# Cross-attention over 16 batches: the steps of the last batches are put in the order of all the others

## The chip, the cores and the metric

The kernel runs on one core of a Trainium2 chip, as one program with one launch. The metric is the device time of that program in microseconds (us), as the median of repeated runs. A profile of one execution stands beside it; its span is the time from the first to the last recorded instruction on the core.

## The reference

There are 16 batches. Each has 256 queries of width 256 (`x`) and 77 context rows of width 192 (`c`). There are 8 heads of width 256, all in fp32.

```
Q = x @ Wq ; K = c @ Wk ; V = c @ Wv               # split into 8 heads
score = Q K^T / sqrt(256), masked keys set to -inf
attn  = softmax(score)                             # over the 77 keys
out   = (attn V, heads side by side) @ Wo + x
result = (out - mean) * rsqrt(var + 1e-5) * gamma + beta     # per row of 256
```

## The kernel before

**Tiling.** A tile is 128 queries; a batch `b` has the two tiles `t = 2b` and `2b+1`, so there are 32 tiles, 0 to 31. The weights are folded ahead of the loop: Wq with Wk per head into `gA`, `gB`, and Wv with Wo per head into `uA`, `uB`. What is left per batch is, on TensorE (PE): `scores` (two tiles, L313), the folded values `vw` of the batch (`prepare_vw`, L241 and L252), the folded keys `a` of a later group of four batches (`prepare_a`, L199 and L213; only while such a group is left), and the weighting of the values by the softmax, which writes the output tile `po`.

**The chain of one tile.** `scores` fills two PSUM banks `ps`. `shift` adds the mask bias on VectorE (DVE), one instruction per bank (L328), and takes the maximum of each head (`top`, L335). `exponential` runs on ScalarE (ACT). `weigh` sums the exponentials (`den`, L355) and inverts the sum (`rden`, L357) on DVE, and multiplies on GpSimd (POOL, L363, two instructions) into a block `p`, of which there are two. `turn` transposes `p` on DVE into `pT` (L373). The weighting matmuls read `pT`. `add_product` adds `po` to the row of `x` on DVE (L483). `finish` takes the statistics (`bn`, L491, and `mv`, L494), `spread` takes the square root on ACT (`std`, L502), and `invert` its inverse on DVE (`rstd`, L509). `normalise` has two forms. By itself it is two DVE instructions (L531, L534). With `aside=True` it is one ACT instruction (L527), which needs a small value `less` from POOL (L513), and two POOL multiplications and additions (`gam` L528, `bet` L529).

**The loop** runs over `b` from -1 to 15. A step issues `scores` of the tiles `new` (batch b+1), the weighting of the tiles `now` (batch b), and the normalisation of the tiles `old` (batch b-1). Each engine runs its instructions in the order in which the code issues them; no scheduler moves them. `NS` is 11.

- For b below `NS` the order is: scores, shift, matmuls of `vw` and `a`; then for each new tile exponential, finish of an old tile, weigh; then the square root, the copies of `vw` and `a` out of PSUM, the weighting with seven products instead of eight (`seven`, L436), a tiny exponential named `warm` that brings ACT's table back to the exponential, invert, normalise, turn, normalise.
- From b = 11 on (batches 12 to 15 being new) the weighting is the plain one (`attend`, L385) and the order is another one. The old tiles are added, finished and square-rooted early in the step, before the new tiles are shifted (after it where b is 11). The maximum is not given to the exponential: POOL subtracts it from the whole tile (L337), and one exponential over 616 elements follows (L346) in place of eight over 77. The `vw` copies stand between the two exponentials, and both tiles are turned at the end of the step.
- After the loop come tiles 28 to 31: 28 and 31 are normalised on DVE, 29 and 30 with `aside`.

PSUM has eight banks in one rotation. From b = 11 on a step takes eight of them: four `ps`, two `pv` (the values, before the copy) and two `po`. The output DMAs are all issued by SyncE (SP), in the order of the code: one for each pair of tiles, and one each for tiles 30 and 31.

Of the kernel before, what the change touches and what calls it, by code (L numbers as in the profile page):

```python
# [10 lines left out]
AF = mybir.ActivationFunctionType  # L11
ALU = mybir.AluOpType
AX = mybir.AxisListType
PSUM = bass.MemoryType.PSUM

P = 128
H = 8
# [36 lines left out]
def kernel(  # L54
# [13 lines left out]
    nc = tc.nc  # L68
    B, S, DI = x.shape
# [5 lines left out]
    QT = S // P  # L75
# [155 lines left out]
    def prepare_vw(b):  # L231

        vw_of[b] = vwp.tile([P, 4, 2, P], F32, tag="vw", name=f"vw_{b}", bufs=3)
        parts = slice(0, 4) if b < NS else slice(1, 5)
        pv = []

        def part_A():
            for k in range(2):
                pv.append(ps_mm.tile([P, 2 * DI], F32, tag="mm", name=f"pv_{b}_{k}"))
                for i in range(NM):  # L240
                    nc.tensor.matmul(  # L241
                        pv[k][i * BK : (i + 1) * BK],
                        cA[:, b, k * BK : (k + 1) * BK],
                        uA[:, parts, :, i],
                        start=True,
                        stop=False,
                    )

        def part_B():
            for i in range(NM):  # L250
                for k in range(2):
                    nc.tensor.matmul(  # L252
                        pv[k][i * BK : (i + 1) * BK],
                        cB[half(k), b, k * BK : (k + 1) * BK],
                        uB[half(k), parts, :, i],
                        start=False,
                        stop=True,
                    )

        def copies():  # L260
            return [
                (vw_of[b][:, :, k, :], pv[k].rearrange("p (q d) -> p q d", q=4)) for k in range(2)
            ]

        return part_A, part_B, copies
# [56 lines left out]
    def shift(t):  # L322


        b, ps = t // QT, ps_of.pop(t)
        s = sp.tile([P, H, S2], F32, tag="s", name=f"s_{t}")
        for a in range(2):
            nc.vector.tensor_tensor(  # L328
                s[:, a * H // 2 : (a + 1) * H // 2],
                ps[a][:, : H // 2 * S2].rearrange("p (h k) -> p h k", k=S2),  # L330
                bias[:, b, :].unsqueeze(1).to_broadcast([P, H // 2, S2]),
                ALU.add,
            )
        top = st.tile([P, H], F32, tag="top", name=f"top_{t}")
        nc.vector.tensor_reduce(top, s, AX.X, ALU.max, negate=t // QT <= NS)  # L335
        if t // QT > NS:
            nc.gpsimd.tensor_tensor(  # L337
                s, s, top.unsqueeze(2).to_broadcast([P, H, S2]), ALU.subtract
            )
        s_of[t] = s, top  # L340

    def exponential(t):
        e = sp.tile([P, H, S2], F32, tag="e", name=f"e_{t}")
        s, top = s_of.pop(t)
        if t // QT > NS:
            nc.scalar.activation(e, s, AF.Exp)  # L346
        else:
            for h in range(H):
                nc.scalar.activation(e[:, h], s[:, h], AF.Exp, bias=top[:, h : h + 1])  # L349
        e_of[t] = e  # L350

    def weigh(t):
# [128 lines left out]
    def add_product(t):  # L481
        y = xg_of[t // GT][:, t % GT, :]
        nc.vector.tensor_tensor(y, po_of.pop(t), y, ALU.add)  # L483

    def finish(t):
        if t in po_of:
            add_product(t)
        g, j = t // GT, t % GT
        y = xg_of[g][:, j, :]
        bn = st.tile([P, 6], F32, tag="bn", name=f"bn_{t}")  # L490
        nc.vector.bn_stats(bn, y)  # L491
        if j == 0:
            mv_of[g] = st.tile([P, GT, 2], F32, tag="mv", name=f"mv_{g}", bufs=2)
        nc.vector.bn_aggr(mv_of[g][:, j, :], bn)  # L494
# [3 lines left out]
    def spread(first, last):  # L498

        g, lo, hi = first // GT, first % GT, (last - 1) % GT + 1  # L500
        std = st.tile([P, GT], F32, tag="std", name=f"std_{first}")
        nc.scalar.activation(std[:, lo:hi], mv_of[g][:, lo:hi, 1], AF.Sqrt, bias=eps)  # L502
        std_of[first, last] = std

    def invert(first, last, aside=False):

        g, lo, hi = first // GT, first % GT, (last - 1) % GT + 1
        rstd = st.tile([P, GT], F32, tag="rstd", name=f"rstd_{first}")
        nc.vector.reciprocal(rstd[:, lo:hi], std_of.pop((first, last))[:, lo:hi])  # L509
        if aside:  # L510
            less = st.tile([P, GT], F32, tag="less", name=f"less_{first}")
            for j in range(lo, hi):
                nc.gpsimd.tensor_scalar(  # L513
                    less[:, j : j + 1], mv_of[g][:, j, 0:1], rstd[:, j : j + 1], -1.0,
                    ALU.mult, ALU.mult,
                )
        for t in range(first, last):
            j = slice(t % GT, t % GT + 1)
            rstd_of[t] = rstd[:, j], less[:, j] if aside else None
# [315 lines left out]

    assert QT == 2
    last = NT - 1
    for b in range(-1, B):
        old = range(max(b - 1, 0) * QT, b * QT)
        now = range(max(b, 0) * QT, (b + 1) * QT)  # L840
        new = range((b + 1) * QT, min(b + 2, B) * QT)
        for t in new:
            scores(t)
        if old and new and b > NS:
            for t in old:
                finish(t)
            spread(old[0], old[-1] + 1)
        for t in new:
            shift(t)
        if b == NS:  # L850
            for t in old:
                finish(t)
            spread(old[0], old[-1] + 1)
        for n in range(0, 2) if b < 0 else range(b + 2, min(b + 3, B // 2)):
            turn_last(n)
        if b >= NS and new:
            invert(old[0], old[-1] + 1, aside=True)
        g, n = (b + 1) // GB + 1, (b + 1) % GB
        work = []
        if b + 1 < B:  # L860
            work.append(prepare_vw(b + 1))
        if g < NG:
            work.append(prepare_a(g, (n,)))
            if n == 0:
                load_xT(g)
                load_x(g)
        for part_A, _, _ in work:
            part_A()
        for _, part_B, _ in work:
            part_B()  # L870
        copies = [copy for _, _, of_part in work for copy in of_part()]
        if b < NS:
            for i, t in enumerate(new):
                exponential(t)
                if old:
                    finish(old[i])
                weigh(t)
            if old:
                spread(old[0], old[-1] + 1)
            for dst, src in copies:  # L880
                nc.scalar.copy(dst, src)
            if b + 1 < NS:
                differences(b + 1)
            if now:
                seven(b)
            nc.scalar.activation(warm, eps, AF.Exp)
            if old:
                invert(old[0], old[-1] + 1)
                normalise(old[0])
            for t in new:  # L890
                turn(t)
            if n >= NF - 2:
                for j in range((n - NF + 2) * GT // 2, (n - NF + 3) * GT // 2, 2):
                    transpose_x(g, j)
            if old:
                normalise(old[1])
            if now:
                add_seven(b)
            if b + 1 < NS:
                sums(b + 1)  # L900
            continue
        for i, t in enumerate(new):
            exponential(t)
            for dst, src in copies[i : i + 1]:
                nc.scalar.copy(dst, src)
        for dst, src in copies[len(new) :]:
            nc.scalar.copy(dst, src)
        for i, t in enumerate(new):
            weigh(t)
            if old and b < B - 2 and i:  # L910
                normalise(old[i])
        for t in now:
            attend(t)
        for t in new:
            turn(t)
        if b < B - 2:
            normalise(old[0], aside=True)
        if b == B - 2:
            for i in range(QT):
                normalise(old[i], aside=True)  # L920
                finish(now[i])
            spread(now[0], now[-1] + 1)

    finish(last - 1)
    spread(last - 1, last)
    invert(last - 3, last - 1, aside=True)
    normalise(last - 3)
    invert(last - 1, last, aside=True)
    for t in range(last - 2, last):
        normalise(t, aside=True)  # L930
    finish(last)
    spread(last, NT)
    invert(last, NT)
# [32 lines left out]
```

## Time and profile before

| what | value |
|---|---|
| median of 3 runs | 284.35 us (283.92 to 285.65) |
| the profiled execution's own time | 285.26 us |
| its span | 283.5 us |
| PE busy | 271.2 us, 96% of the span |
| DVE busy | 207.5 us, 73% |
| POOL busy | 179.6 us, 63% |
| ACT busy | 156.8 us, 55% |

The page lists busy times, the span in 40 slices, the chain of work that ended last, and the costliest groups of instructions by line. A group row gives the count, the total, the mean of one in ns, and the idle time of its engine just before it with what ended it. A timeline row gives the start and length of an instruction, or of several merged ones, in us from the span's start. A merged or pipelined length can overlap the next start a little.

### The profile page before, as it was taken

Reading aid. Unit: us, or ns where it says so; the run is one execution under the profiler, and the core shown is the slowest. Engines: PE = TensorE matmul, PEld = TensorE weight load, DVE = VectorE, ACT = ScalarE, POOL = GpSimd, SP = SyncE. Lnnn points to the kernel's source line nnn. Section 1 sums busy time; section 2 is a strip of 40 time slices with the busy share of each in tenths; the row PEclk is TensorE's granted clock in tenths of the full one; section 3 lists DMA queues with packets and bytes.
Section 4 is the critical chain, followed back from the end, with each engine's and each line's share of the span. In section 5 each row is a group of like instructions: output and inputs, shape, how many; then the busy total and the mean of one; then the engine's idle time right before and its main releaser. Section 6 shows DMA issues by size and latency. Waiting matters only on the chain.

```text
span 283.5 us, 13229 instructions
## 1 busy us (share of the span) xinstructions
PE 271.2 (96%) x5925; PEld 196.8 (69%) x5925; DVE 207.5 (73%) x421; ACT 156.8 (55%) x390; POOL 179.6 (63%) x240
## 2 busy tenths in 40 slices
PE   7899999999999999999999999999999999999970
PEld 7756589985585859586858595959595957568440
DVE  0245762678738888878788888787888868898882
ACT  3212142147547676767676767676768834725641
POOL 1000049955677777787877777878777556748574
PEclk9999999999999999999999999999999999999996
DMA  5997899940000000940100009401010101010112
GB/s 186 239 225 170 258 291 232 169 133 3 2 6 2 25 19 27 201 152 3 42 2 28 16 17 214 152 5 41 4 39 4 39 5 39 3 39 5 39 38 74
DMA packets 35640, 22.60 MB, mean 80 GB/s; under 512 B 17712, under 2 KB 34048, under 8 KB 35584
## 3 DMA queue, kind: packets, MB, share of 16 engines
q1 hardware_dynamic: 35584, 21.77, 30.1%
q8 instruction: 46, 0.75, 1.1%
q14 instruction: 10, 0.08, 0.1%
HBM read 17.57 MB, written 4.19 MB: 77 GB/s over the span
## 4 chain that ended last, share of the span: by engine, by line
PE 77%; DVE 11%; POOL 4%; DMA 2%; ACT 2%; issue 2%; POOLq 0%; SPq 0%
PE ps L313 19%; PE pa L199 12%; PE po L436 9%; PE pv L241 7%; PE pm L436 7%; PE pa L213 6%; PE pv L252 4%; PE pu L683 3%; PE pr L274 2%; DMA wq_nat<-in_L_xattn_Wq_dram 2%; DVE top L335 2%; DVE s L328 2%; DVE bn L491 2%; DVE pT L373 2%; POOL p L363 1%
## 5 line engine op out<-in xcount | busy, mean ns | idle before, releaser
L349 ACT ACTIVATE e<-s,top 128x77 f32<-128x77 f32 x192 | 50.3, 346 | 42.9 <-DVE top L335 40.7
L313 PE MATMUL ps<-a,xT 128*32 128x154 f32 x2048 | 70.1, 294 | 0.0
L313 PEld LDWEIGHTS ps<-a,xT 128*32 128x32 f32 x2048 | 66.3, 110 | 1.6 <-issue 0.7
L363 POOL TENSOR_TENSOR p<-e,rden 128x512 f32<-128x512 f32 x64 | 46.7, 752 | 27.3 <-DVE rden L357 24.2
L328 DVE TENSOR_TENSOR s<-ps,bias 128x308 f32<-128x308 f32 x64 | 29.7, 473 | 14.8 <-PE ps L313 13.1
L199 PE MATMUL pa<-cA,gA 128*32 128x308 f32 x512 | 35.9, 423 | 0.4 <-ACT cA L151 0.4
L469 POOL TENSOR_TENSOR xg<-xg,m 128x256 f32<-128x256 f32 x33 | 24.2, 733 | 13.8 <-DVE xg L483 12.1
L199 PEld LDWEIGHTS pa<-cA,gA 128*32 128x32 f32 x512 | 17.0, 110 | 20.5 <-issue 7.0
L241 PE MATMUL pv<-uA,cA 128*32 128x512 f32 x256 | 30.6, 592 | 0.0
L355 DVE TENSOR_REDUCE den<-e 128x8 f32<-128x616 f32 x32 | 24.8, 776 | 7.2 <-ACT e L346 4.8
L373 DVE STREAM_TRANSPOSE pT<-p 128x640 f32<-128x640 f32 x32 | 25.5, 825 | 2.8 <-POOL p L363 2.8
L335 DVE TENSOR_REDUCE top<-s 128x8 f32<-128x616 f32 x32 | 25.4, 795 | 1.1
L671 POOL COPY cB<-cB 64x224 f32<-64x224 f32 (+1 forms) x6 | 1.9, 358 | 37.3 <-DVE cB L153 37.3
L399 POOL TENSOR_TENSOR ts<-vw 128x768 f32<-128x768 f32 x11 | 22.0, 2001 | 0.0
L385 PE MATMUL po<-vw,pT 128*32 128x256 f32 x320 | 19.2, 380 | 0.5 <-DVE pT L373 0.5
L213 PE MATMUL pa<-cB,gB 64*32 64x308 f32 x512 | 19.5, 420 | 0.0
L502 ACT ACT_TABLE_LOAD x15 | 19.2, 1283 | 0.3
L213 PEld LDWEIGHTS pa<-cB,gB 64*32 64x32 f32 x512 | 9.7, 107 | 11.3 <-issue 7.6
L337 POOL TENSOR_TENSOR s<-s,top 128x616 f32<-128x616 f32 x8 | 9.7, 1217 | 12.2 <-DVE top L335 11.0
L252 PE MATMUL pv<-uB,cB 64*32 64x512 f32 x256 | 17.4, 601 | 0.0
L385 PEld LDWEIGHTS po<-vw,pT 128*32 128x32 f32 x320 | 10.3, 110 | 10.0 <-DVE s L328 2.5
L531 DVE SCALAR_TENSOR_TENSOR xg<-xg,mv,gam 128x256 f32<-128x256 f32 x25 | 16.8, 671 | 0.0
(116 smaller groups left out, 474.7 us busy)
## 6 DMA issues: line engine op xcount, KB each, us to landing
xT<-in_x_dram SPq DMA_DIRECT2D x16, 256.0 KB, 5.7
xg<-in_x_dram SPq DMA_DIRECT2D x4, 1024.0 KB, 7.4
out_dram<-xg SPq DMA_DIRECT2D x15, 256.0 KB, 2.4
wo<-in_L_xattn_Wo_dram SPq DMA_DIRECT2D x4, 512.0 KB, 5.4
wvT<-in_L_xattn_Wv_dram SPq DMA_DIRECT2D x16, 96.0 KB, 4.0
wq_nat<-in_L_xattn_Wq_dram SPq DMA_DIRECT2D x2, 512.0 KB, 6.8
wq_blk<-in_L_xattn_Wq_dram SPq DMA_DIRECT2D x8, 128.0 KB, 4.3
wk_blk<-in_L_xattn_Wk_dram SPq DMA_DIRECT2D x8, 96.0 KB, 6.2
```

The costliest lines, as they stand in the source:

```text
L199: nc.tensor.matmul(flat(o[i * BK : (i + 1) * BK]), gA[:, h, cols(dc, i)], flat(cA[:, batches, :]), start=not B_first, stop=B_first,)
L213: nc.tensor.matmul(flat(banks[j + k][i * BK : (i + 1) * BK]), gB[half(k), h % NF, cols(dc, i)], flat(cB[half(k), batches, :]), start=B_fir ...
L241: nc.tensor.matmul(pv[k][i * BK : (i + 1) * BK], cA[:, b, k * BK : (k + 1) * BK], uA[:, parts, :, i], start=True, stop=False,)
L252: nc.tensor.matmul(pv[k][i * BK : (i + 1) * BK], cB[half(k), b, k * BK : (k + 1) * BK], uB[half(k), parts, :, i], start=False, stop=True,)
L313: nc.tensor.matmul(ps[m // 2][i * BK : (i + 1) * BK, m % 2 * 2 * S2 : (m % 2 + 1) * 2 * S2], xT_of[g][:, j * NM + m, dc], flat(a_of[g][:, ...
L328: nc.vector.tensor_tensor(s[:, a * H // 2 : (a + 1) * H // 2], ps[a][:, : H // 2 * S2].rearrange("p (h k) -> p h k", k=S2), bias[:, b, :]. ...
L335: nc.vector.tensor_reduce(top, s, AX.X, ALU.max, negate=t // QT <= NS)
L349: nc.scalar.activation(e[:, h], s[:, h], AF.Exp, bias=top[:, h : h + 1])
L363: nc.gpsimd.tensor_tensor(part, e_mh[:, :, :, keys], rden_mh.unsqueeze(3).to_broadcast(list(part.shape)), ALU.mult,)
L373: nc.vector.transpose(pT_of[t].rearrange("p n m q -> p m n q"), p.rearrange("p m (n k) -> p m n k", k=BK),)
L385: nc.tensor.matmul(po[i * BK : (i + 1) * BK], pT[:, n, i], vw_of[b][:, 2 - n // 2 * 2 : 4 - n // 2 * 2, n % 2, :] if n < NF else vr[:, b, ...
L436: nc.tensor.matmul(out[i * BK : (i + 1) * BK], weight[:, i], moving, start=(n == 0), stop=(n == len(terms) - 1),)
```

## The change

The steps with b from 11 to 14 take the order of the steps below 11, with `attend` in the place of `seven`. In them the negated maximum goes into the exponential as its bias, eight instructions per tile, and the subtraction on POOL is gone. Of the two old tiles one is normalised with `aside` and the other on DVE, as before; which of them comes first is exchanged with the order. `invert` makes `less` only for tiles normalised aside. A `warm` exponential follows in steps 11 to 13. `add_product` of the two current tiles moves to the end of the step, and their statistics to the next one. Step 14 keeps both old tiles aside and finishes the current ones. Step 15 becomes code after the loop: `attend` of tiles 30 and 31, and the end for tiles 28 to 31, of which again 28 and 31 go to DVE and 29 and 30 aside, but tile 29 is started before tile 30 is finished.

```diff
@@ shift, exponential
-        nc.vector.tensor_reduce(top, s, AX.X, ALU.max, negate=t // QT <= NS)
-        if t // QT > NS:
-            nc.gpsimd.tensor_tensor(
-                s, s, top.unsqueeze(2).to_broadcast([P, H, S2]), ALU.subtract
-            )
+        nc.vector.tensor_reduce(top, s, AX.X, ALU.max, negate=True)
...
-        if t // QT > NS:
-            nc.scalar.activation(e, s, AF.Exp)
-        else:
-            for h in range(H):
-                nc.scalar.activation(e[:, h], s[:, h], AF.Exp, bias=top[:, h : h + 1])
+        for h in range(H):
+            nc.scalar.activation(e[:, h], s[:, h], AF.Exp, bias=top[:, h : h + 1])
@@ the loop
-        if old and new and b > NS:
-            for t in old:
-                finish(t)
-            spread(old[0], old[-1] + 1)
...
-        if b == NS:
-            for t in old:
-                finish(t)
-            spread(old[0], old[-1] + 1)
...
-        if b >= NS and new:
-            invert(old[0], old[-1] + 1, aside=True)
...
+        for i, t in enumerate(new):
+            exponential(t)
+            if old:
+                finish(old[i])
+            weigh(t)
+        if old:
+            spread(old[0], old[-1] + 1)
+        for _, _, copies in work:
+            for dst, src in copies():
+                nc.scalar.copy(dst, src)
...
-        for i, t in enumerate(new):
-            exponential(t)
-            for dst, src in copies[i : i + 1]:
-                nc.scalar.copy(dst, src)
-        for dst, src in copies[len(new) :]:
-            nc.scalar.copy(dst, src)
-        for i, t in enumerate(new):
-            weigh(t)
-            if old and b < B - 2 and i:
-                normalise(old[i])
         for t in now:
             attend(t)
-        for t in new:
-            turn(t)
         if b < B - 2:
+            invert(old[0], old[-1] + 1, aside=old[:1])
             normalise(old[0], aside=True)
-        if b == B - 2:
-            for i in range(QT):
-                normalise(old[i], aside=True)
-                finish(now[i])
+            nc.scalar.activation(warm, eps, AF.Exp)
+            turn(new[0])
+            normalise(old[1])
+            turn(new[1])
+            for t in now:
+                add_product(t)
+        else:
+            turn(new[0])
+            invert(old[0], old[-1] + 1, aside=old)
+            for t in old:
+                normalise(t, aside=True)
+            turn(new[1])
+            for t in now:
+                finish(t)
             spread(now[0], now[-1] + 1)
@@ after the loop
+    for t in new:
+        attend(t)
+    invert(last - 3, last - 1, aside=(last - 2,))
+    normalise(last - 2, aside=True)
     finish(last - 1)
     spread(last - 1, last)
-    invert(last - 3, last - 1, aside=True)
     normalise(last - 3)
-    invert(last - 1, last, aside=True)
-    for t in range(last - 2, last):
-        normalise(t, aside=True)
+    invert(last - 1, last, aside=(last - 1,))
+    normalise(last - 1, aside=True)
     finish(last)
     spread(last, NT)
     invert(last, NT)
```

More of the change, by code (lines that the diff above doesn't have):

```diff
@@ L503, in spread, with invert @@
         std_of[first, last] = std
-    def invert(first, last, aside=False):
+    def invert(first, last, aside=()):
         g, lo, hi = first // GT, first % GT, (last - 1) % GT + 1
@@ L511, in invert @@
             less = st.tile([P, GT], F32, tag="less", name=f"less_{first}")
-            for j in range(lo, hi):
+            for j in (t % GT for t in aside):
                 nc.gpsimd.tensor_scalar(
@@ L837 @@
     last = NT - 1
-    for b in range(-1, B):
+    for b in range(-1, B - 1):
         old = range(max(b - 1, 0) * QT, b * QT)
         now = range(max(b, 0) * QT, (b + 1) * QT)
-        new = range((b + 1) * QT, min(b + 2, B) * QT)
+        new = range((b + 1) * QT, (b + 2) * QT)
         for t in new:
             scores(t)
-        if old and new and b > NS:
-            for t in old:
-                finish(t)
-            spread(old[0], old[-1] + 1)
         for t in new:
             shift(t)
-        if b == NS:
-            for t in old:
-                finish(t)
-            spread(old[0], old[-1] + 1)
         for n in range(0, 2) if b < 0 else range(b + 2, min(b + 3, B // 2)):
             turn_last(n)
-        if b >= NS and new:
-            invert(old[0], old[-1] + 1, aside=True)
         g, n = (b + 1) // GB + 1, (b + 1) % GB
-        work = []
-        if b + 1 < B:
-            work.append(prepare_vw(b + 1))
+        work = [prepare_vw(b + 1)]
         if g < NG:
@@ L870 @@
             part_B()
-        copies = [copy for _, _, of_part in work for copy in of_part()]
-        if b < NS:
-            for i, t in enumerate(new):
-                exponential(t)
-                if old:
-                    finish(old[i])
-                weigh(t)
-            if old:
-                spread(old[0], old[-1] + 1)
-            for dst, src in copies:
-                nc.scalar.copy(dst, src)
-            if b + 1 < NS:
-                differences(b + 1)
+        for i, t in enumerate(new):
[8 more added lines that the diff above has]
+                nc.scalar.copy(dst, src)
+        if b + 1 < NS:
+            differences(b + 1)
+        if b < NS:
             if now:
@@ L901 @@
             continue
-        for i, t in enumerate(new):
-            exponential(t)
-            for dst, src in copies[i : i + 1]:
-                nc.scalar.copy(dst, src)
-        for dst, src in copies[len(new) :]:
-            nc.scalar.copy(dst, src)
-        for i, t in enumerate(new):
-            weigh(t)
-            if old and b < B - 2 and i:
-                normalise(old[i])
         for t in now:
             attend(t)
-        for t in new:
-            turn(t)
         if b < B - 2:
+            invert(old[0], old[-1] + 1, aside=old[:1])
             normalise(old[0], aside=True)
-        if b == B - 2:
-            for i in range(QT):
-                normalise(old[i], aside=True)
-                finish(now[i])
+            nc.scalar.activation(warm, eps, AF.Exp)
[12 more added lines that the diff above has]
+                finish(t)
             spread(now[0], now[-1] + 1)
+    for t in new:
+        attend(t)
+    invert(last - 3, last - 1, aside=(last - 2,))
+    normalise(last - 2, aside=True)
     finish(last - 1)
     spread(last - 1, last)
-    invert(last - 3, last - 1, aside=True)
     normalise(last - 3)
-    invert(last - 1, last, aside=True)
-    for t in range(last - 2, last):
-        normalise(t, aside=True)
+    invert(last - 1, last, aside=(last - 1,))
+    normalise(last - 1, aside=True)
     finish(last)
```

## The prediction

> **What bounds the kernel now.** I read the busy times by stage first, because the change leaves everything before 224 us alone. The stages are the four steps with b = 11 to 14, cut where PE starts the scores of a new batch, and the end. The columns are the stretch, its length, then busy time and count of PE, PE's weight loads, DVE, ACT and POOL, the granted clock, the DMA share and GB/s.
>
> ```profile
> 224.30:235.70 11.40, 11.40 (x252) 7.40 (x246) 7.88 (x20) 6.01 (x11) 6.15 (x9) 1.00 0.08 26
> 235.70:247.05 11.35, 11.35 (x245) 7.36 (x241) 9.55 (x22) 5.80 (x9) 7.74 (x12) 1.00 0.08 26
> 247.05:258.43 11.38, 11.38 (x246) 7.36 (x241) 10.10 (x22) 5.84 (x9) 7.38 (x11) 1.00 0.08 26
> 258.43:269.81 11.38, 11.38 (x244) 7.22 (x236) 10.05 (x22) 5.85 (x9) 7.39 (x11) 1.00 0.08 27
> 269.81:283.50 13.69, 4.70 (x84) 3.02 (x80) 7.46 (x21) 3.23 (x7) 8.51 (x13) 0.84 0.16 57
> ```
>
> PE has no gap in the four steps: 11.37 us each, and no order on the other engines can make them shorter. What can change is whether PE is kept waiting, and the last 13.7 us. The next view is the timeline of PE and DVE where PE first waits.
>
> ```profile
> 269.37 0.61 PE L385 MATMUL po<-vr,pT 128*32 128x256 f32 x8
> 270.52 1.93 PE L385 MATMUL po<-vw,pT 128*32 128x256 f32 x32 [0.54 <-DVE pT L373]
> ...
> 269.53 0.84 DVE L373 STREAM_TRANSPOSE pT<-p 128x640 f32<-128x640 f32 x1
> 271.05 0.84 DVE L373 STREAM_TRANSPOSE pT<-p 128x640 f32<-128x640 f32 x1 [0.67 <-POOL p L363]
> ```
>
> The weighting of tile 30 starts 0.54 us late, as its transpose ends at 270.37. DVE is late because its own round is full: its first L328 of a step starts at 240.55 and 251.84, that is 4.9 and 4.8 us after PE began those scores at 235.67 and 247.04, though the first bank can be read after about 1.3. So in the before, DVE trails PE by about 3.5 us in the last steps. The third view is the end, on POOL and SP.
>
> ```profile
> 275.00 1.24 POOL L513 TENSOR_SCALAR less<-mv,rstd 128x1 f32<-128x1 f32 x3 [0.98 <-DVE rstd L509]
> 276.65 0.72 POOL L528 TENSOR_TENSOR xg<-xg,gam 128x256 f32<-128x256 f32 x1 [0.41 <-ACT xg L527]
> 277.45 0.95 POOL L529 TENSOR_TENSOR xg<-xg,bet 128x256 f32<-128x256 f32 x1
> 278.37 0.90 POOL L528 TENSOR_TENSOR xg<-xg,gam 128x256 f32<-128x256 f32 x1
> 279.35 0.72 POOL L529 TENSOR_TENSOR xg<-xg,bet 128x256 f32<-128x256 f32 x1
> ...
> 280.09 0.83 SPq L536 DMA_DIRECT2D out_dram<-xg  x2
> ```
>
> POOL stood idle 0.98 us for DVE's `rstd` of tiles 28 and 29 and then did tiles 29 and 30 in a row to 280.07. The two last DMA issues end at 280.92, and the span ends 2.58 us later. DVE was done with tile 31 at 278.69, so POOL's row of two tiles sets the end.
>
> The last view gives the order that the change brings in, as it already runs at b = 10 (PE began those scores at 210.19):
>
> ```profile
> 213.96 4.20 ACT L349 ACTIVATE e<-s,top 128x77 f32<-128x77 f32 x16 [3.52 <-DVE top L335]
> 218.18 1.28 ACT L502 ACT_TABLE_LOAD   x1
> 219.47 0.30 ACT L502 ACTIVATE std<-mv,eps 128x2 f32<-128x2 f32 x1
> ...
> 219.37 1.56 POOL L363 TENSOR_TENSOR p<-e,rden 128x512 f32<-128x512 f32 x2 [0.44 <-DVE rden L357]
> ...
> 219.80 0.17 DVE L509 RECIPROCAL rstd<-std 128x2 f32<-128x2 f32 x1 [0.58 <-ACT std L502]
> 219.89 0.82 DVE L531 SCALAR_TENSOR_TENSOR xg<-xg,mv,gam 128x256 f32<-128x256 f32 x1
> ```
>
> Counted from the start of the scores: exponentials from 3.77 to 7.97, `rden` of the second tile done at 9.03, `rstd` at 9.6, second `p` done at 10.74.
>
> **What the Trainium skill says.** "ScalarE: Activation LUTs", section "What ACT_TABLE_LOAD costs", gives 1283 ns for a load and 1380 ns of drain after it, and for an activation with a pointer bias 280 ns plus 0.833 ns per element, with back-to-back ones overlapping by 93 ns. For 77 elements that is 344 ns, or 251 ns apart. The trace has loads of 1283 ns, exponentials of 346 ns, and 16 of them in 4.20 us, 262 ns apart. A drain isn't seen: at 231.46 a load of 1.28 us is followed by the exponential at 232.75. The section "Table sets: the hidden batching unit" says that exp and sqrt lie in different sets and that cheap functions lie in every set. That agrees: no load stands ahead of a copy (L905) or the L527 identity. "SBUF — State Buffer", section "Who interferes with whom", says that a DVE instruction with two SBUF inputs contends with a GpSimd instruction that reads SBUF. The trace has this for L534: 0.49 us alone (236.05), 1.16 us beside `p` on POOL (247.31). PSUM inputs as in L483 and L328 aren't touched by it.
>
> **Part by part.** Per step b = 11 to 14:
>
> *Removed on POOL:* two subtractions of 1.22 us (L337) and one or two `less` of about 0.25. They stood on DVE's way to the exponential: top done, 1.23 on POOL, then the exponential.
>
> *Added on ACT:* 16 exponentials in 4.20 us for two of 0.72, so 2.8 us more. The table loads stay two per step (one in b = 14), moved. ACT's sum is 4.2 + 1.28 + 0.3 + two copies 1.05 + 0.6 + 1.28 + 0.2 = 8.9 us, below PE's 11.37. The `warm` load ends at about 11.0 (`less`) + 0.6 + 1.5 = 13.1, and the next exponential is due at 11.37 + 3.77 = 15.1, so it is hidden by 2 us; without that cover it would cost at most 1.5 per step.
>
> *Moved on DVE:* the instructions stay the same in kind and number. After `rstd` at 9.6 come turn 0.8 (10.5), L531 0.82 beside `p` (11.2), L534 0.48 (11.7; POOL has only `less` left until ACT has done L527), turn 0.8 (12.5), two additions 0.75 (13.3). So DVE is free for the next scores 1.9 us after PE starts them. The second bank comes at 2.34 (226.63 in the row of b = 11), and the first addition takes 0.38. It fits with nothing to spare: I take a lag of 0 per step, with bounds -0.1 and +0.7 (L534 at 1.16 instead of 0.48), over three steps at most 2.0.
>
> *Copies of `vw` later on ACT:* behind `std`, done at about 10.6 instead of 10.1. Their banks are needed by the next `pv` at 11.37 + 4.2 = 15.6, so nothing.
>
> *Output DMAs:* the same count and order on SP. Where a pair waits for POOL, nothing but later output stands behind it.
>
> *Step 14 and the end,* from scores at 258.42. Exponentials end at 266.39, turn of tile 30 at 268.2, `p` of 31 at 269.16, turn of 31 at 270.05. PE then starts tile 30 at 269.98 without the 0.54 us wait, and `po` of 31 is done about 0.5 earlier, at 274.5. POOL after 269.16: `less` of 26 and 27 0.5 (269.66), L527 0.6 (270.3), four L528/L529 at before's 3.05 for the four (273.35), `less` of 29 0.4 (273.75), L527 0.6 (274.4), two operations 1.75 (276.2), `less` of 30 0.3 (276.5), L527 0.6 (277.1), two operations 1.7 (278.9). Before, this was 280.07: 1.2 us earlier. DVE's tile 31 has `std` queued on ACT behind L527 of tile 30, which waits for that late `less`: 277.0 + 0.3, `rstd` 0.2, L531 0.47, L534 0.83 beside POOL, 278.8. So both ends meet at 278.9, two issues 0.83, then 2.58: the span is 282.3 instead of 283.5.
>
> The sum is -1.2 us on the profiled execution: 285.26 to 284.06. That execution lies 0.9 above the median, so I put the same difference on the median: 284.35 - 1.2 = 283.1.
>
> **Rivals.**
>
> *Given back (about 284.5).* The saved time is lost to the shared reads of DVE and POOL: L534 at 1.16 in each step gives a lag up to 2.0 by the end, 283.1 + 2.0 = 285.1 at worst, some 284.5 in the middle. For it: the before shows 1.16 in two steps out of three. Against: in the new order L534 starts after `p` is done.
>
> *Slower (about 287.5).* The new order has run only at 14.1 us per step, where PE also does `a`; the round shift, exponentials, `den`, `p`, turn, additions, next shift may need more than 11.37. Its place is DVE's first L328 in steps 12 to 14; each us of excess costs three us at the end, since POOL's last row hangs on `p` of tile 31. An excess of 1.5 gives 4.5 - 1.2 = +3.3. It decides from an excess of 0.4 (no gain left), and by 1% from 1.35. Against it: the sum above ends at 13.3, while that would need 14.7; what it would take is both L531 and L534 held for a whole `p`, besides a late `std`.
>
> *Clearly faster (about 281.2).* If POOL kept up, DVE's tile 31 alone would end it: `po` at 274.5, addition, statistics, `std`, `rstd`, two L531/L534, together 2.6, 277.1; 0.83 and 2.58 make 280.5, a gain of 3.0. Against it: after 269.66 POOL still has eight `gam`/`bet` operations of 0.73 or more, 5.8 us without a single wait, and the waits for L527 and `less` between them.
>
> *That the change doesn't do what it says* I exclude: the instruction order of the changed kernel shows the 16 exponentials, no subtraction, and the turns split around L531.
>
> **Chances.** Forecast 0.60; given back 0.20; slower 0.12; clearly faster 0.08. About 1% is what a measurement of this kernel can tell from no change, 2.8 us. The forecast and the rival given back lie within it: 0.80 same, 0.08 faster, 0.12 slower. The forecast's own bounds are 281.9 (POOL's last six operations uncontended at 0.73, and short `less`) to 283.5; with half of the faster case left out, and the given-back case taken in, the range is 281.7 to 285.2.
>
> **What would show it.** Right: PE busy without a gap to the end of the weighting of tile 31; DVE's first L328 about 1.9 to 2.3 us after each scores start from b = 12 on; 16 exponentials in 4.2 us; POOL busy from 269 on with the last `bet` at about 278.9, and std of tile 31 behind L527 of tile 30. Wrong: the first L328 drifting from step to step, PE waiting for `pT`, or POOL idle in the last 8 us while DVE or ACT is late.

## The result, and the profile after

The changed kernel takes 282.59 us (282.41 to 282.80, 5 runs) where the kernel before takes 284.49 us (283.92 to 285.65, 5 runs). The ratio is 0.9931, with a 95% interval of 0.9908 to 0.9954. It is faster by 1.9 us, or 0.7%, which lies inside the 1% called no change in the prediction; the interval of the ratio does not contain 1. The forecast was 283.1, a gain of 1.2 us.

The profiled execution has a span of 280.8 us, 2.7 less than before. Not all of that is the change: PE began the scores of batch 12 at 223.55 here and at 224.29 before, and up to there the two kernels run the same instructions. Counted from that point, before takes 283.5 - 224.29 = 59.21 us and after 280.8 - 223.55 = 57.25 us, so the changed part gained 1.96 us (the spans are given to 0.1 us), close to the 1.9 us of the medians. To compare with a time of before on one clock, 0.74 is added to a time of after.

The timeline of PE after, at the place where it waited for the transpose of tile 30 before:

```profile
268.62 0.61 PE L378 MATMUL po<-vr,pT 128*32 128x256 f32 x8
269.06 1.91 PE L378 MATMUL po<-vw,pT 128*32 128x256 f32 x32
```

There is no wait any more. 269.06 is 269.80 on the clock of before, where the same matmuls started at 270.52. The reason is on VectorE (L328 keeps its line, L373 has become L366, and L531 and L534 have become L524 and L527):

```profile
233.24 0.82 DVE L366 STREAM_TRANSPOSE pT<-p 128x640 f32<-128x640 f32 x1
233.99 0.45 DVE L524 SCALAR_TENSOR_TENSOR xg<-xg,mv,gam 128x256 f32<-128x256 f32 x1
234.47 0.48 DVE L527 SCALAR_TENSOR_TENSOR xg<-xg,rstd,bet 128x256 f32<-128x256 f32 x1
...
236.27 0.46 DVE L328 TENSOR_TENSOR s<-ps,bias 128x308 f32<-128x308 f32 x1
237.27 0.48 DVE L328 TENSOR_TENSOR s<-ps,bias 128x308 f32<-128x308 f32 x1 [0.54 <-PE ps L313]
...
259.01 0.46 DVE L328 TENSOR_TENSOR s<-ps,bias 128x308 f32<-128x308 f32 x1
260.02 0.48 DVE L328 TENSOR_TENSOR s<-ps,bias 128x308 f32<-128x308 f32 x1 [0.55 <-PE ps L313]
```

The first L328 comes 1.34 us after PE began those scores (234.93), and 1.33 us in the step of batch 15 (257.68). VectorE now waits for PE, by half a microsecond in each step. The same instructions before:

```profile
225.59 0.48 DVE L328 TENSOR_TENSOR s<-ps,bias 128x308 f32<-128x308 f32 x1
...
240.55 0.83 DVE L328 TENSOR_TENSOR s<-ps,bias 128x308 f32<-128x308 f32 x2
...
247.31 1.16 DVE L534 SCALAR_TENSOR_TENSOR xg<-xg,rstd,bet 128x256 f32<-128x256 f32 x1
...
263.12 0.83 DVE L328 TENSOR_TENSOR s<-ps,bias 128x308 f32<-128x308 f32 x2
```

Before, the first L328 came 1.30 us after the scores of batch 12 (224.29), 4.88 after those of batch 13 (235.67), 4.79 after those of batch 14 (247.04) and 4.70 after those of batch 15 (258.42). So the lag came in between two batches and was then held: VectorE's round of 11.29 us was a little shorter than PE's 11.37, but not short enough to win the lag back. What L534 was before is L527 now: 1.16 us in two of three steps before, 0.48 in every step after, because `p` is finished when it starts.

The timelines of GpSimd, ScalarE and SyncE at the end (L528 and L529 have become L521 and L522, L513 has become L506, L502 has become L495):

```profile
266.84 1.38 POOL L356 TENSOR_TENSOR p<-e,rden 128x512 f32<-128x512 f32 x2 [0.42 <-DVE rden L350]
...
272.20 0.27 POOL L506 TENSOR_SCALAR less<-mv,rstd 128x1 f32<-128x1 f32 x1
273.19 0.89 POOL L521 TENSOR_TENSOR xg<-xg,gam 128x256 f32<-128x256 f32 x1 [0.72 <-ACT xg L520]
274.15 0.72 POOL L522 TENSOR_TENSOR xg<-xg,bet 128x256 f32<-128x256 f32 x1
274.85 0.26 POOL L506 TENSOR_SCALAR less<-mv,rstd 128x1 f32<-128x1 f32 x1
275.83 0.72 POOL L521 TENSOR_TENSOR xg<-xg,gam 128x256 f32<-128x256 f32 x1 [0.72 <-ACT xg L520]
276.63 0.78 POOL L522 TENSOR_TENSOR xg<-xg,bet 128x256 f32<-128x256 f32 x1
...
275.15 0.60 ACT L520 ACTIVATE xg<-xg,less,rstd 128x256 f32<-128x256 f32 x1 [1.86 <-POOL less L506]
275.66 0.28 ACT L495 ACTIVATE std<-mv,eps 128x1 f32<-128x1 f32 x1
...
277.44 0.83 SPq L529 DMA_DIRECT2D out_dram<-xg  x2
```

The row no longer stands idle for `rstd` of tiles 28 and 29. It now waits twice for 0.72 us, each time for the round `less`, L520, `gam`. It ends at 277.41, on the clock of before at 278.15 against 280.07, and the two DMA issues follow at once.

The row as a whole did not become shorter; it starts sooner. Before, the last `p` on GpSimd is the end of this row:

```profile
268.11 2.90 POOL L363 TENSOR_TENSOR p<-e,rden 128x512 f32<-128x512 f32 x4
```

Counted from the scores of batch 15, `p` of tile 31 was done at 12.59 us before (271.01 - 258.42) and is done at 10.54 after (268.22 - 257.68), 2.05 sooner. From there to the last `bet` it took 9.06 us before and takes 9.19 after. Of the 3.37 us by which the first L328 of batch 15 comes sooner, 2.05 reach `p`; the way from L328 to `p` is 9.21 us instead of 7.89, and 0.95 of it are VectorE's two waits for PE's banks (0.55 and 0.40).

### The profile page after: what moved, and what is told of

Same layout as the page of the kernel before. It is cut to its first block, busy times and chain, and to the rows that moved or that the text cites. A ratio compares the mean times of both kernels' runs of the same rounds, so it can differ in the third digit from the quotient of the medians.

```text
span 280.8 us, 13274 instructions
## 1 busy us (share of the span) xinstructions
PE 270.8 (96%) x5925; PEld 195.6 (70%) x5925; DVE 206.1 (73%) x421; ACT 166.5 (59%) x447; POOL 168.2 (60%) x228
## 4 chain that ended last, share of the span: by engine, by line
PE 89%; POOL 2%; ACT 2%; DMA 2%; DVE 2%; issue 0%; SPq 0%; ACTq 0%; POOLq 0%
PE ps L313 23%; PE pa L199 12%; PE pv L241 9%; PE po L429 9%; PE pm L429 7%; PE pa L213 6%; PE pv L252 5%; PE po L378 5%; PE pu L676 3%; PE pr L274 2%; DMA wq_nat<-in_L_xattn_Wq_dram 2%; ACT e L342 1%; PE pg L719 1%; PE pgb L676 1%; PE pw L690 1%; PE pr L284 1%
## 5 line engine op out<-in xcount | busy, mean ns | idle before, releaser
L342 ACT ACTIVATE e<-s,top 128x77 f32<-128x77 f32 x256 | 67.1, 346 | 52.1 <-DVE top L335 49.9
L356 POOL TENSOR_TENSOR p<-e,rden 128x512 f32<-128x512 f32 x64 | 45.8, 738 | 46.6 <-DVE rden L350 46.4
L328 DVE TENSOR_TENSOR s<-ps,bias 128x308 f32<-128x308 f32 x64 | 30.3, 475 | 17.6 <-PE ps L313 15.9
L199 PEld LDWEIGHTS pa<-cA,gA 128*32 128x32 f32 x512 | 16.4, 110 | 21.1 <-issue 7.6
L366 DVE STREAM_TRANSPOSE pT<-p 128x640 f32<-128x640 f32 x32 | 25.6, 824 | 2.4 <-POOL p L356 2.4
L861 ACT COPY vw<-pv 128x512 f32<-128x512 f32 x32 | 16.9, 578 | 2.5 <-PE pv L252 2.5
L495 ACT ACT_TABLE_LOAD x14 | 18.0, 1283 | 0.3
L524 DVE SCALAR_TENSOR_TENSOR xg<-xg,mv,gam 128x256 f32<-128x256 f32 x25 | 17.1, 682 | 0.0
L861 ACT COPY a<-pa 128x308 f32<-128x308 f32 x48 | 16.6, 446 | 0.0
```

Of the source, the lines that this page charges most:

```text
L199: nc.tensor.matmul(flat(o[i * BK : (i + 1) * BK]), gA[:, h, cols(dc, i)], flat(cA[:, batches, :]), start=not B_first, stop=B_first,)
L328: nc.vector.tensor_tensor(s[:, a * H // 2 : (a + 1) * H // 2], ps[a][:, : H // 2 * S2].rearrange("p (h k) -> p h k", k=S2), bias[:, b, :]. ...
L356: nc.gpsimd.tensor_tensor(part, e_mh[:, :, :, keys], rden_mh.unsqueeze(3).to_broadcast(list(part.shape)), ALU.mult,)
L366: nc.vector.transpose(pT_of[t].rearrange("p n m q -> p m n q"), p.rearrange("p m (n k) -> p m n k", k=BK),)
```

## The experiments

The theory: the new order of the steps ends VectorE's lag behind PE, so the row of work on GpSimd begins sooner; the form of the exponential and the order of the last four tiles matter little. The rivals: the order of the last tiles gained it; the subtraction taken off GpSimd gained it; the gain is given back by contention. In the table, "end" is the span less the time at which PE began the scores of batch 15, in the profiled execution of each kernel, so that the part ahead of the change does not enter. "`p` of 31" is the time at which GpSimd has done `p` of tile 31, counted from the same scores.

| kernel | median us | ratio to before (95% interval) | `p` of 31, us | end us |
|---|---|---|---|---|
| before | 284.49 | 1 | 12.59 | 25.08 |
| the change | 282.59 | 0.9931 (0.9908 to 0.9954) | 10.54 | 23.12 |
| x1, last tiles alone | 284.09 | 0.9986 (0.9972 to 0.9999) | 12.60 | 24.73 |
| x2, steps alone | 282.63 | 0.9925 (0.9906 to 0.9944) | 10.54 | 23.33 |
| x3, subtraction in the new order | 282.56 | 0.9919 (0.9900 to 0.9938) | 10.38 | 23.09 |
| x4, bias in the old order | 294.88 | 1.0358 (1.0335 to 1.0381) | see there | see there |
| x5, square root of 31 first | 282.62 | 0.9944 (0.9925 to 0.9962) | 10.54 | 23.28 |
| x6, `less` of 30 early | 281.58 | 0.9908 (0.9892 to 0.9924) | 10.54 | 22.34 |
| x7, as x6, tile 27 on VectorE | 281.96 | 0.9917 (0.9904 to 0.9930) | 10.72 | 22.69 |
| x8, contended L524 | 282.44 | 0.9932 (0.9919 to 0.9946) | 10.53 | 23.07 |
| x9, no `warm` | 284.64 | 1.0013 (1.0003 to 1.0023) | 12.78 | 25.35 |

The end follows `p` of tile 31: less that time it is 12.49 us before, 12.58 after and 12.57 in x9. Only x6 and x7, which change the row behind `p`, are clearly below it, and x1, which does so too, a little (12.13).

**x1 and x2: the halves of the change.** x1 is the kernel before with the new code after the loop (`invert` takes the tiles for `less` as a list):

```diff
...
+    invert(last - 3, last - 1, aside=(last - 2,))
+    normalise(last - 2, aside=True)
     finish(last - 1)
     spread(last - 1, last)
-    invert(last - 3, last - 1, aside=True)
     normalise(last - 3)
-    invert(last - 1, last, aside=True)
-    for t in range(last - 2, last):
-        normalise(t, aside=True)
+    invert(last - 1, last, aside=(last - 1,))
+    normalise(last - 1, aside=True)
     finish(last)
```

> The kernel before, with only the code after the loop taken from the change (tile 29 started before tile 30 is finished, its less made apart). Theory (the new steps end VectorE's lag, and the end is worth little by itself): PE still waits 0.54 us for the transpose of tile 30, the first L328 of a step still trails by 4.8 us; GpSimd's last row starts about 1.2 us sooner but then waits for the less of tile 30, and VectorE's tile 31 waits behind tile 30 on ScalarE: about -0.5 us against before (ratio 0.998). Rival (the end is what gained): about -1.5 us or more (0.995 or less).

x2 is the changed kernel with this diff taken back.

> The changed kernel, with the code after the loop as in the kernel before. Theory: no PE wait, first L328 of each step 1.3 us after its scores, and about -1.9 us against before (0.9933), within 0.3 us of the changed kernel. Rival (the end is what gained): at most -0.7 us (0.9975).

x1 gained 0.14%, about 0.4 us, x2 0.75%. PE in x1:

```profile
269.27 1.93 PE L385 MATMUL po<-vw,pT 128*32 128x256 f32 x32 [0.54 <-DVE pT L373]
```

The 0.54 us wait is there as before, `p` of tile 31 is as late as before, and x1 ends with tile 31 on VectorE. In x2 `p` is as early as in the change. So the steps carry the gain, and the order of the last tiles adds nothing that can be measured to them. In x2 GpSimd waits 0.49 us, makes three `less` in a row (1.24 us), waits 0.41 and then runs four operations without a wait to 277.51; in the change it has two waits of 0.72. Counted from the scores of batch 15 the rows end at 19.94 and 19.73.

Which of the moves within a step ends the lag was not tried one by one. The traces let one see a part of it: before, VectorE adds and takes the statistics of two tiles between the last transposition and L328 (238.58 to 240.63, 2.05 us), after, only two additions stand there (235.63 to 236.34, 0.71 us).

**x3 and x4: the form of the exponential.** x3 is the changed kernel with the old form from batch 12 on:

```diff
-        nc.vector.tensor_reduce(top, s, AX.X, ALU.max, negate=True)
+        nc.vector.tensor_reduce(top, s, AX.X, ALU.max, negate=t // QT <= NS)
+        if t // QT > NS:
+            nc.gpsimd.tensor_tensor(
+                s, s, top.unsqueeze(2).to_broadcast([P, H, S2]), ALU.subtract
+            )
...
+        if t // QT > NS:
+            nc.scalar.activation(e, s, AF.Exp)
+        else:
+            for h in range(H):
...
```

> The changed kernel, but from batch 12 on with the maximum subtracted on GpSimd and one exponential of 616 elements per tile, as before. Theory (it is the order, not the form of the exponential): subtraction 1.22 and exponential 0.72 take as long as eight exponentials of 2.1 us, so within 0.4 us of the changed kernel, -1.5 to -2.2 us against before (0.992 to 0.995). Rival (the gain is the subtraction taken off GpSimd and off VectorE's shared reads): most of it goes, -0.7 us or less (0.9975 or more).

It is as fast as the change, 0.9919 against 0.9931. In the new order the subtraction on GpSimd costs nothing that can be measured.

x4 takes this diff the other way, in the kernel before.

> The kernel before, but with the maximum as bias and eight exponentials per tile in batches 12 to 15; the order of the steps is unchanged. Theory: the second tile's exponentials end about 1 us later than before in each step, VectorE's round of 11.3 us, which has no slack in this order, grows by up to 1 us, and the lag is carried on over three steps: +1 to +3 us (1.004 to 1.011). Rival (the subtraction was the cost): -1 us or better (0.9965 or less).

The sign was right and the size was not: +10.4 us, more than three times the upper end of what was expected. The table load before, on ScalarE:

```profile
240.98 1.28 ACT L346 ACT_TABLE_LOAD   x1
243.54 0.72 ACT L346 ACTIVATE e<-s 128x616 f32<-128x616 f32 x1 [1.27 <-POOL s L337]
```

ScalarE, VectorE and PE in x4:

```profile
242.63 0.30 ACT L495 ACTIVATE std<-mv,eps 128x2 f32<-128x2 f32 x1 [3.82 <-DVE mv L487]
244.27 1.28 ACT L342 ACT_TABLE_LOAD   x1 [1.35 <-DVE top L335]
245.56 2.11 ACT L342 ACTIVATE e<-s,top 128x77 f32<-128x77 f32 x8
247.58 0.57 ACT L898 COPY vw<-pv 128x512 f32<-128x512 f32 x1
248.04 2.11 ACT L342 ACTIVATE e<-s,top 128x77 f32<-128x77 f32 x8
...
242.51 0.83 DVE L328 TENSOR_TENSOR s<-ps,bias 128x308 f32<-128x308 f32 x2
...
279.30 3.64 PE L378 MATMUL po<-vw,pT 128*32 128x256 f32 x32 [6.56 <-DVE pT L366]
```

Two things add up in a step. The exponentials and the copy between them run from 245.56 to 250.15, 4.59 us after the load, where before the way from the end of the first `top` (242.20) through the subtractions to the end of the second exponential (245.86) was 3.66. That is the microsecond I had counted. And the table load now stands in the way: before, it ran right behind `std`, at 240.98, while the exponential waited for GpSimd. In the timeline of x4 the load itself carries the wait for `top`, so it starts when `top` is done, and its 1.28 us come on top. The loads start at 244.27 and, one step on, at 257.89, so a round takes 13.62 us where it took 11.29 before (L328 at 240.55 and 251.84). 2.33 us of excess in each step are carried on, and PE waits 6.56 us for the transpose of tile 30, besides 1.26 and 1.85 in the steps before. My 1 us in that expectation missed the load. It also missed the step of batch 12, where the load stands ahead of the exponential in both kernels: there the two exponentials and the copy between them take 4.58 us in x4 (231.95 to 236.53) and 1.81 before (232.75 to 234.56), and the first L328 of batch 13 is 2.77 us later than before. 2.77 and three times 2.33 are 9.8 of the 10.4 us. The times of x4 from the scores of batch 15 (`p` of 31 at 21.03, the end at 34.46) can't be compared with the others, as these scores themselves start late; from the scores of batch 12 it takes 69.92 us and before 59.21.

**x9: the load in the new order.** The change keeps the load away by `warm`. x9 takes it out:

```diff
-            nc.scalar.activation(warm, eps, AF.Exp)
             turn(new[0])
```

> The changed kernel without the tiny exponential (warm) at the end of steps 11 to 13. Theory: the table load for the exponential then waits together with the first exponential for the maximum, as in the run with the bias in the old order, and costs 1.35 us in steps 12, 13 and 14. VectorE has 0.6 us to spare per step: the second bank's addition is late by 0.75 in step 13 and 1.5 in step 14, p of tile 31 by 2.8, and the kernel takes about +2.8 us against the changed one (about 1.003 against before). Rival (PE sets the pace, ScalarE has room): within 0.5 us of the changed kernel (0.993 to 0.995).

Against the change it costs 1.0013/0.9931, 0.8% or 2.3 us by the ratios, and 25.35 - 23.12 = 2.2 us by the profiles: more than the whole gain, and less than the 2.8 us expected.

```profile
238.23 1.28 ACT L342 ACT_TABLE_LOAD   x1 [3.46 <-DVE top L335]
239.52 4.11 ACT L342 ACTIVATE e<-s,top 128x77 f32<-128x77 f32 x16
...
250.14 1.28 ACT L342 ACT_TABLE_LOAD   x1 [2.83 <-DVE top L335]
...
248.38 0.85 DVE L328 TENSOR_TENSOR s<-ps,bias 128x308 f32<-128x308 f32 x2
...
260.30 0.85 DVE L328 TENSOR_TENSOR s<-ps,bias 128x308 f32<-128x308 f32 x2
```

ScalarE is idle 3.46 us and then loads; the load could have run in that time. VectorE's round becomes 11.92 us (248.38 to 260.30), 0.55 more than PE's 11.37, and the lag adds up over the steps. The addition for the second bank is late by 0.55 us in step 13 and 1.09 in step 14, where 0.75 and 1.5 were expected, and `p` of tile 31 by 2.24, which is what the end loses. This is the rival called slower in the prediction: once the round is longer than PE's, the excess of each step is carried to the end, past a slack of about 0.6 us.

**x8: contention put in.** The changed kernel with VectorE's normalising ahead of both transposes:

```diff
-            turn(new[0])
             normalise(old[1])
+            turn(new[0])
             turn(new[1])
```

> The changed kernel, with VectorE's two normalising instructions ahead of both transposes in steps 11 to 13, so that L524 runs beside p on GpSimd. L524 goes from 0.45 to 0.8 us. Theory: VectorE has about 0.6 us to spare per step before it is late for the second bank, so the time stays within 0.2 us of the changed kernel, with the first L328 at 1.7 instead of 1.3 us after its scores. Rival (the gain is given back by contention): 0.4 us late per step, carried on over three steps, +1.0 us or more.

L524 went to 0.82 us in all three steps, and the time stayed: 0.9932, end 23.07.

```profile
233.48 0.82 DVE L524 SCALAR_TENSOR_TENSOR xg<-xg,mv,gam 128x256 f32<-128x256 f32 x1
...
236.87 0.46 DVE L328 TENSOR_TENSOR s<-ps,bias 128x308 f32<-128x308 f32 x1
237.52 0.48 DVE L328 TENSOR_TENSOR s<-ps,bias 128x308 f32<-128x308 f32 x1 [0.19 <-PE ps L313]
```

VectorE still waits 0.19 us for the second bank, where it waited 0.54. The slack takes in the 0.37 us that L524 became longer.

**x5, x6 and x7: what sets the end.** In x5 ScalarE takes the square root of tile 31 ahead of tile 30's L520:

```diff
-    normalise(last - 1, aside=True)
     finish(last)
     spread(last, NT)
+    normalise(last - 1, aside=True)
     invert(last, NT)
```

> The changed kernel, with the square root of tile 31 put ahead of tile 30's L520 on ScalarE. If that queueing sets the end, VectorE's rstd of tile 31 comes at 275.1 instead of 276.0 on the changed kernel's clock and the kernel gains up to 0.9 us. If GpSimd's row sets it (bet of tile 30 at 277.41, and the two last DMA issues behind it on SyncE), VectorE ends a us earlier and the time stays within 0.3 us of the changed kernel (ratio to before 0.992 to 0.995).

```profile
275.67 0.96 POOL L521 TENSOR_TENSOR xg<-xg,gam 128x256 f32<-128x256 f32 x1 [0.72 <-ACT xg L520]
...
275.57 0.48 DVE L527 SCALAR_TENSOR_TENSOR xg<-xg,rstd,bet 128x256 f32<-128x256 f32 x1
...
276.71 0.72 POOL L522 TENSOR_TENSOR xg<-xg,bet 128x256 f32<-128x256 f32 x1
...
277.46 0.83 SPq L529 DMA_DIRECT2D out_dram<-xg  x2
```

Counted from the scores of batch 15, VectorE is done at 18.53 instead of 20.02 us, and nothing is gained: the DMAs stand behind GpSimd's last `bet`, at 19.91 instead of 19.73, since `gam` of tile 30 now runs beside VectorE and takes 0.96 instead of 0.72. The chain of waits of the changed kernel ends on VectorE; that engine was last by 0.3 us and was not what held the end: the issue for tile 31 stands behind that for tile 30 on SyncE and starts at 277.89, after VectorE's 277.70.

x6 makes `less` of tile 30 between `gam` and `bet` of tile 29:

```diff
             nc.gpsimd.tensor_tensor(y, y, gam, ALU.mult)
+            if between:
+                between()
             nc.gpsimd.tensor_tensor(y, y, bet, ALU.add)
...
-    normalise(last - 2, aside=True)
-    finish(last - 1)
-    spread(last - 1, last)
-    normalise(last - 3)
-    invert(last - 1, last, aside=(last - 1,))
+
+    def while_29():
+        finish(last - 1)
+        spread(last - 1, last)
+        normalise(last - 3)
+        invert(last - 1, last, aside=(last - 1,))
+
+    normalise(last - 2, aside=True, between=while_29)
```

> The changed kernel, with less of tile 30 made between gam and bet of tile 29, so that ScalarE's L520 of tile 30 runs beside bet of tile 29. Theory (GpSimd's row of gam, bet, less sets the end): the row loses 0.7 us of waiting and the end comes 0.7 to 1.0 us sooner (about 0.990 against before). Rival (VectorE's tile 31 or the DMA issues set it): within 0.3 us of the changed kernel.

```profile
273.73 0.26 POOL L506 TENSOR_SCALAR less<-mv,rstd 128x1 f32<-128x1 f32 x1
273.95 0.72 POOL L524 TENSOR_TENSOR xg<-xg,bet 128x256 f32<-128x256 f32 x1
274.70 0.72 POOL L521 TENSOR_TENSOR xg<-xg,gam 128x256 f32<-128x256 f32 x1
275.50 0.78 POOL L524 TENSOR_TENSOR xg<-xg,bet 128x256 f32<-128x256 f32 x1
```

The second wait of 0.72 us is gone, since L520 of tile 30 runs beside `bet` of tile 29. The end comes 0.78 us sooner than in the change, and with 281.58 us (0.9908) it is the fastest kernel here. The intervals of x6 and the change overlap a little; the trace shows where the time went.

x7 adds to x6 that tile 27 is normalised on VectorE in step 14.

```diff
             turn(new[0])
-            invert(old[0], old[-1] + 1, aside=old)
-            for t in old:
-                normalise(t, aside=True)
+            invert(old[0], old[-1] + 1, aside=old[:1])
+            normalise(old[0], aside=True)
+            normalise(old[1])
             turn(new[1])
```

> As the run before (less of tile 30 between gam and bet of tile 29), and tile 27 normalised on VectorE in the idle 0.8 us ahead of the transpose of tile 31, two operations less in GpSimd's row. Theory: tile 29's gam then starts when rstd of tile 28 allows, 0.6 us sooner than 273.19, and the end comes 1.0 to 1.5 us before that of the changed kernel (about 0.988 to 0.990). Rival (the row is not what ends last): no better than the run before it, or worse by the 0.1 to 0.5 us that the transpose of tile 31 is late.

This expectation failed, and its rival came true: 0.9917, end 22.69, 0.35 later than x6. The intervals of x6 and x7 overlap, so what follows is read from the traces alone. GpSimd has two operations less and is then idle until VectorE delivers `rstd` of tiles 28 and 29:

```profile
271.79 0.26 POOL L506 TENSOR_SCALAR less<-mv,rstd 128x1 f32<-128x1 f32 x1 [0.96 <-DVE rstd L502]
272.77 0.87 POOL L521 TENSOR_TENSOR xg<-xg,gam 128x256 f32<-128x256 f32 x1 [0.72 <-ACT xg L520]
274.09 0.27 POOL L506 TENSOR_SCALAR less<-mv,rstd 128x1 f32<-128x1 f32 x1 [0.45 <-DVE rstd L502]
...
273.09 0.83 DVE L529 SCALAR_TENSOR_TENSOR xg<-xg,rstd,bet 128x256 f32<-128x256 f32 x1
```

VectorE's own work is late, as tile 27 now stands ahead of the transposition of tile 31: the first L526 of tile 28 starts 15.19 us after the scores of batch 15 (272.60 - 257.41) and in x6 at 14.83 (272.19 - 257.36). `gam` of tile 29 then meets tile 28 on VectorE (L529 0.83 instead of 0.48 in x6), so `rstd` of tile 30 is late and GpSimd waits 0.45 for it. With the row this short, VectorE holds it.

## Why the prediction was right, and where its size was off

- **PE keeps its 11.37 us per step; the gain is in VectorE's lag and in the end.** Shown. The end is the only stretch that became shorter, and it became so because `p` of tile 31 is done 2.05 us sooner.
- **VectorE late before "because its own round is full".** Only in part. A round of 11.29 us against PE's 11.37 could not win the lag back, but it did not make it either: the lag fell from 4.88 to 4.70 us. The old order had put it there once, between batches 12 and 13.
- **The 0.54 us wait goes.** Shown in the profile after, and it stays in x1.
- **VectorE free 1.9 us after the scores begin, with nothing to spare.** Too late by 0.56: it was 1.34. I had charged L531 at 0.82 us beside `p`. The first transpose stands between in the new order, and `p` took 1.38 instead of 1.56, so L524 began as `p` ended and took 0.45: 0.37 of the 0.56; the rest is in rounded lengths. The slack is about 0.6 us, not zero: the second bank comes at 2.34, two additions in a row start 0.39 apart (248.38 and 248.77 in x9), and 2.34 - 0.39 - 1.34 = 0.61. x8 shows that even 0.82 would have fitted.
- **`warm` hidden by 2 us, at most 1.5 per step without it.** Its end was put at 13.1 after the scores and the next exponential at 15.1; measured are 236.71 - 223.55 = 13.16 and 238.67 - 223.55 = 15.12. Without it, x9 lost 2.2 us in all three steps, less than the bound.
- **The end at 278.9 on the clock of before.** It was 278.15, and this 0.75 is why 1.2 became 1.9. The step of the sum that was mis-sized is GpSimd's row. Counted from the scores of batch 15: second `p` done at 10.54 (I had 10.74), first `gam` at 11.50 (11.88), fourth operation done at 14.54 (14.93), `gam` of 29 at 15.51 (15.98), its `bet` done at 17.19 (17.78), `bet` of 30 done at 19.73 (20.48). I had taken the contended rows of before for `p` (1.56) and for each last pair (1.75 and 1.7, measured 1.68 and 1.58), and a first hop from `less` to `gam` of 1.14 us that takes 0.96, as L520 starts when the first of two `less` is done. The sum also has a slip of 0.1 in it (277.1 and 1.7 are 278.8).
- **Both ends meet.** VectorE ended at 277.70 and GpSimd at 277.41. x5 shows that GpSimd's held the end.
- **The rivals.** Given back by contention: it did not happen, as L527 took 0.48 us in every step; x8 shows that 0.37 us more per step costs nothing. The 0.68 of the prediction was not tried; against the slack of 0.6 it leaves under 0.1 per step, an estimate. Slower: it did not happen, but x9 shows the mechanism, and that it was one small instruction away. Clearly faster: GpSimd's row kept it out; x6 gains 0.78 us by shortening the row, and x7 nothing more, as VectorE then holds it.
- **Readings that were off without harm.** L534 at 236.05 was not alone: the second `p` began at 236.21 beside it, and it was `p` that became longer, 1.24 us instead of 1.05. The `vw` copies are not later: the second ended 10.74 us after the scores before (235.03 - 224.29), 10.1 being its start, and ends at 10.53 after. The exponentials of a tile start 0.25 us apart; 262 ns was 4.20 us divided by 16, with the length of the last one and the step between the tiles in it.
- **What the hit is worth.** The range of 281.7 to 285.2 us contains the time of the kernel before as well: a change without any gain would have fallen into it too. What speaks for the forecast is the lag that went, the wait that went, and the two halves x1 and x2.

## What to carry to other kernels

Where PE has no gap and the other engines run their own round beside it, look at two things. One is the length of that round. If it is longer than PE's, each step's excess is carried on to the end (2.33 us in x4, 0.55 us in x9); if it is shorter, a delay that fits into the slack costs nothing (0.37 us in x8). The other is the lag. A round that is no longer than PE's can still trail far behind, as in the kernel before (11.29 against 11.37 us, and 4.7 to 4.9 us behind the scores). In the steps of that kernel it cost nothing; it was paid once, at the end, where the last row of work hung on it.

In x4 and x9 the table load cost time because it waited together with the activation that needs it; a tiny activation of the same kind ahead of the wait put the load into idle time. At the end of a kernel look for hops between engines in the row that ends last, and put the small operation that starts the hop ahead of a large one, as in x6.

## What was not expected of the hardware

The table load is not always early. In the kernel before it ran at 240.98, 2.6 us ahead of its exponential at 243.54; in x4 and x9 it started only when `top` was done and stood 1.28 us in the way. In the kernel before the exponential waited for GpSimd, in x4 and x9 for VectorE; no run here shows what decides whether the load waits too. The Trainium skill's "ScalarE: Activation LUTs", section "What ACT_TABLE_LOAD costs", has the 1283 ns, which every load here took. The 1380 ns of drain that it adds per switch shows nowhere: in x9 the exponentials start 0.01 us after the load ends (238.23 + 1.28, then 239.52).
